# A fused attention kernel gets a new opening: loads reordered, biases transposed beside the token, batch 0 projected by seven products

## The chip, the cores and the metric

The kernel runs on one core of a Trainium2 chip. The metric is the device time of one execution in microseconds, as the median of several runs. A core has five engines that run side by side, each through its own list of instructions in order: TensorE (PE: matmuls and transposes, results into PSUM), ScalarE (ACT: exp, copies), VectorE (DVE: adds, maxima, copies), GpSimd (POOL) and SyncE (SP, which here only issues DMAs). PSUM has eight banks of 128 x 512 fp32. An engine that needs another's result waits on a semaphore.

## The reference

Eight batches of 512 tokens with 512 features, 16 heads of 32. One attention layer with a residual; a condition token of each batch is added to all queries and keys.

```python
Q = _split_heads(x @ Wq.T + bq)
K = _split_heads(x @ Wk.T + bk)
V = _split_heads(x @ Wv.T + bv)
tQ = _split_heads(tokens @ Wq.T + bq)
tK = _split_heads(tokens @ Wk.T + bk)
cQ = Q + tQ
cK = K + tK
scores = jnp.einsum('bhqd,bhkd->bhqk', cQ, cK) / jnp.sqrt(jnp.float32(HEAD_DIM))
attn = jax.nn.softmax(scores, axis=-1)
out = jnp.einsum('bhqk,bhkd->bhqd', attn, V)
...
x = x + _L0_cond_ref(x, cond_1024[:, None, :], ...)
```

Since both the token's and the tokens' projections carry the bias, each query and key gets the token's projection plus twice the bias. The kernel keeps that sum in `tok`.

## The kernel before

Work is cut into 32 steps t: a batch b (8) and a group g of four heads (4 per batch). The operands are fp32. For each t the kernel makes transposed queries and keys (`qkT`, 128 features of the group by 512 tokens), then for each of four row blocks qc the scores of four heads (`row_scores`, four matmuls of 32 x 512 that share the array), their negated row maxima (`row_max_of`, VectorE) and the softmax denominators (`denominators`: four exps on ACT that sum along the row). The maxima of a whole step are split into three bf16 parts (`split_max`, POOL), transposed (`transpose_max`) and added to the transposed scores as a matmul with ones (`exponentials`), whose exps are then multiplied by V (`weighted`).

The order on TensorE, ACT, VectorE and POOL is the order of the text (`manual_schedule`). In the kernel before, that is switched on behind the memsets and loads; only the opening and what follows is written out by hand. Banks are dealt out by the table `TURNS`: each quarter of a step uses one row of it, `advance()` goes to the next row. `one()` deals banks round in the opening.

The loop over t has four quarters. Each has one `exponentials(t, kc)`, one `row_max` of the next step, its `denominators`, and some of the work for the next batch, so that batch b + 1 is loaded, transposed and projected while batch b is in the softmax.

Projections come in two kinds. `project_qk` and `project_v` are four matmuls of 128 x 512 accumulated in one bank. `first_products` and `other_products` do two groups of q or k (or two chunks of V) at once by a Strassen-Winograd scheme: a 2 x 2 block product with seven block products instead of eight, each two matmuls of 256 columns. They need sums of blocks of the weights (`combine_w`, four sums of 128 x 512 per matrix on POOL, into `wc`) and sums of blocks of x (`combine_x`, four sums, on VectorE, into `xc`). `first_products` does products 1, 6, 2 (half) and 7, and ACT copies product 1 (`m1`) out of PSUM ahead of the denominators it is given (`dens`); `other_products` does 4, 5, the other half of 2, and 3. In the kernel before, batch 0 is projected by `project_qk` and `project_v`, and the seven products start with batch 1.

The opening in its order: 28 bf16 matmuls on ones while the loads come; then for c = 0 to 3 a tile of x transposed and a block of w_q transposed (`transpose_w`; even blocks leave PSUM by ACT, odd ones by VectorE); the token transposed (`condT`); projection q of t = 0; `condition("q")` (the token through Wq); w_k's blocks transposed; `condition_end("q")` (turning the result back and adding the biases); projection k with `condition("k")` in between; half of w_v; then four quarters of "burst" (`burst_of_maxima`) in which t = 0's maxima and denominators are interleaved with the other projections of batch 0, the transposes of batch 1's x and the rest of w_v. `combine_w` stands behind the fourth burst. `transpose_x(n)` also loads x tile n + 4. x_7 is transposed by the opening and once more by the loop at t = 0.

Loads before: SyncE issues the token, x_0 to x_3, w_k, the two biases (as 128 x 4, one number at a time), the broadcast bv, w_v; ACT's queue issues w_q.

Of the kernel before, what the change touches and what calls it, by code (L numbers as in the profile page):

```python
# [17 lines left out]
def kernel(  # L18
# [34 lines left out]
    P = 128  # L53
# [38 lines left out]
        (2, 5, 3, 4, 6, 7, 0, 1),  # L92
    ]
# [19 lines left out]
    def load_x(n):  # L113

        if n < B * NS:
            xs[n] = xp.tile([P, D], F32, tag="x", name=f"x_{n}")
            nc.sync.dma_start(xs[n], x[n // NS, n % NS * P : (n % NS + 1) * P, :])
# [14 lines left out]
    for n in ("v", "q", "k"):  # L132
        ws[n] = stage.tile([P, NC, D], F32, tag="w", name=f"w_{n}")

    def load_w(n, w, queue):
        wv = w.rearrange("(c p) d -> p c d", p=P)
        for c in range(NC):
            queue.dma_start(ws[n][:, c, :], wv[:, c, :])

    cond_sb = const.tile([B, D], F32, tag="cond", name="cond_sb")  # L140
    nc.sync.dma_start(cond_sb, cond)
    for n in range(NS):
        load_x(n)
    load_w("q", Wq, nc.scalar)
    load_w("k", Wk, nc.sync)
    bqk = const.tile([P, 2, NC], F32, tag="bqk", name="bqk")
    nc.sync.dma_start(bqk[:, 0, :], bq.rearrange("(c p) -> p c", p=P))
    nc.sync.dma_start(bqk[:, 1, :], bk.rearrange("(c p) -> p c", p=P))
    bvb = const.tile([P, D], F32, tag="bvb", name="bvb")
    nc.sync.dma_start(bvb, bv.rearrange("(o d) -> o d", o=1).broadcast_to([P, D]))  # L150
    load_w("v", Wv, nc.sync)
# [4 lines left out]
    identb = const.tile([P, P], BF16, tag="identb", name="identb")  # L156
    nc.vector.tensor_copy(identb, ident)
    ones = const.tile([P, P], F32, tag="ones", name="ones")
    nc.vector.memset(ones, 1.0)
    onesb = const.tile([P, P], BF16, tag="onesb", name="onesb")  # L160
    nc.vector.memset(onesb, 1.0)
# [6 lines left out]
    nc.vector.memset(condT, 0.0)  # L168
    xc = const.tile([P, 4, 2, HS], F32, tag="xc", name="xc")
# [7 lines left out]
    def transpose_w(n, dc, pt):  # L177

        for cc in range(NC):
            nc.tensor.transpose(  # L180
                pt[:, cc * P : (cc + 1) * P], ws[n][:, dc, cc * P : (cc + 1) * P], ident
            )
        o = wT[n][:, :, dc * P : (dc + 1) * P]
        pv = pt.rearrange("p (c s) -> p c s", c=NC)
        if n == "q":
            if dc % 2:
                nc.vector.tensor_scalar(o, pv, SCALE, None, ALU.mult)
            else:
                nc.scalar.activation(o, pv, AF.Copy, scale=SCALE)
        elif dc % 2:  # L190
            nc.vector.tensor_copy(o, pv)
        else:
            nc.scalar.copy(o, pv)
# [37 lines left out]
    def combine_x(b, half):  # L231

        if b >= B:
            return
        blk = [[xT[b][:, i * 2 : i * 2 + 2, j * HS : (j + 1) * HS] for j in range(2)] for i in range(2)]
        to = [xc[:, i, :, :] for i in range(4)]
        if half == 0:
            nc.vector.tensor_tensor(to[2], blk[1][1], blk[0][1], ALU.subtract)
            nc.vector.tensor_tensor(to[1], to[2], blk[0][0], ALU.add)
        else:  # L240
            nc.vector.tensor_tensor(to[0], blk[0][1], blk[0][0], ALU.subtract)
            nc.vector.tensor_tensor(to[3], blk[1][0], to[1], ALU.subtract)
# [34 lines left out]

    def project_v(n, pt):
        b, sc = divmod(n, NS)
        for cc in range(NC):  # L280
            nc.tensor.matmul(  # L281
                pt,
                xT[b][:, cc, sc * P : (sc + 1) * P],
                wT["v"][:, cc, :],
                start=(cc == 0),
                stop=(cc == NC - 1),
            )
        nc.vector.tensor_copy(vs[b % 2][:, sc, :], pt)
# [60 lines left out]
    def first_products(n, b, u, dens, small, at):  # L349
# [3 lines left out]
        one_, two_ = banks(0), banks(at)  # L353
# [241 lines left out]
    def condition_end(n, pt):  # L595
# [10 lines left out]
        if n == "q":  # L606
            nc.vector.tensor_scalar(bqk[:, 0, :], bqk[:, 0, :], SCALE, None, ALU.mult)
        b1 = bqk[:, i, :].unsqueeze(2).broadcast_to([P, NC, B])
        nc.vector.tensor_tensor(sum4, sum4, b1, ALU.add)
        nc.vector.tensor_tensor(tok[:, i], sum4, b1, ALU.add)  # L610


    ctx.enter_context(
        tc.manual_schedule(
            engines={
                mybir.EngineType.PE,
                mybir.EngineType.Activation,
                mybir.EngineType.DVE,
                mybir.EngineType.Pool,
            }  # L620
        )
    )

    warm = one()
    for _ in range(28):
        nc.tensor.matmul(warm[:, :P], onesb, onesb, start=True, stop=True)
    for c in range(NS):
        transpose_x(c, one())
        transpose_w("q", c, one())
        if c == 1:  # L630
            pc = one()
            for cc in range(NC):
                nc.tensor.transpose(
                    pc[:, cc * B : (cc + 1) * B], cond_sb[:, cc * P : (cc + 1) * P], ident[:B, :B]
                )
            nc.vector.tensor_copy(
                condT[:, :, 0:B], pc[:, : NC * B].rearrange("p (c b) -> p c b", b=B)
            )
    pq = one()
    for cc in range(NC):  # L640
        project_qk_part(0, "q", cc, pq)
    condition("q", one())
    for c in range(NC):
        transpose_w("k", c, one())
    condition_end("q", one())
    project_qk_end(0, "q", pq)
    condition("k", one())
    pk = one()
    for cc in range(NC):
        project_qk_part(0, "k", cc, pk)  # L650
        if cc == 1:
            condition_end("k", one())
    project_qk_end(0, "k", pk)
    transpose_w("v", 0, one())
    transpose_w("v", 1, one())
    turn[0] = 3
# [4 lines left out]
    def burst_of_maxima(t, qc):  # L661
        row_max(t, qc)
        if qc == NS - 1:
            split_max(t)
        denominators(t, qc)

    burst_of_maxima(0, 0)
    project_qk(1, "q", banks(1))
    advance()
    burst_of_maxima(0, 1)  # L670
    project_qk(1, "k", banks(1))
    advance()
    burst_of_maxima(0, 2)
    transpose_w("v", 2, banks(0))
    transpose_w("v", 3, banks(1))
    transpose_x(NS, banks(2))
    project_qk(2, "q", banks(3))
    advance()
    burst_of_maxima(0, 3)
    for n in ("v", "q", "k"):  # L680
        combine_w(n)
    transpose_x(NS + 1, banks(0))
    project_v(0, banks(3))
    transpose_x(NS + 2, banks(1))
    project_qk(2, "k", banks(2))
    advance()
    burst_of_maxima(1, 0)
    project_v(1, banks(3))
    transpose_max(0, banks(1))
    transpose_x(NS + 3, banks(2))  # L690
    project_qk(3, "q", banks(0))
    load_residual(0)
    advance()
# [26 lines left out]
    for t in range(T - 3):  # L720
# [9 lines left out]
        else:  # L730
            transpose_x(t + NS + 3, banks(0), nc.scalar.copy)
            if t:
                project_pair("q", *qk_of, dens, nothing, (1, 3))
            else:
                dens()
                project_qk(3, "k", banks(1))
# [4 lines left out]
        denominators(t + 1, 2)  # L741
        if t:
            invert(t - 1, sums[t - 1])
            weighted(t - 1, banks(0))
        else:
            project_v(2, banks(0))
# [12 lines left out]
        else:  # L759
            dens()  # L760
            project_v(3, banks(0))
# [162 lines left out]
```

## Time and profile before

| | |
|---|---|
| median of the runs | 768.01 us (767.38 to 769.47, 3 runs) |
| profiled execution | 768.58 us |
| its span, first to last instruction | 766.8 us |
| mean granted TensorE clock | 0.997 |
| TensorE busy | 755.3 us, 99% |
| ACT busy | 626.7 us, 82% |
| VectorE busy | 521.6 us, 68% |
| POOL busy | 127.2 us, 17% |
| DMA | 29.76 MB, 38 GB/s over the span |

Times in the views are in microseconds from the start of the span. A line of the timeline has the start, the time covered, the engine, the line of the kernel, the operation, output and inputs, and the shape. An fp32 matmul appears as two records; x8 on a line is four matmuls. The time covered of a TensorE line ends with a modelled tail, so that the next line can start a little earlier; the step from start to start is what a piece of work costs. A window line has from:to, its length, then busy time and instructions of TensorE, of its weight loads (PEld), of VectorE, ACT and POOL, then the granted clock, the DMA share and GB/s.

### The profile page before, as it was taken

The page shows a single profiled execution, that of the slowest core. Times are in us where ns is not written, and L with a number is a line of the kernel's source. Part 1 is how long each engine was busy: PE and PEld are TensorE (multiplying, and loading weights), DVE is VectorE, ACT ScalarE, POOL GpSimd, SP SyncE. Part 2 cuts the span into 40 slices and gives each one's busy share as a digit, 9 for nine tenths or more (in the row PEclk, how much of TensorE's full clock was granted, in tenths as well). Part 3 has the DMA queues.
Part 4 walks back from the last instruction along what each step waited for, and adds up shares of the span by engine and source line. Part 5 has one row for each costly group of instructions (what it writes and reads, how often), then busy time and mean ns, then how long its engine had stood idle before and what let it go on. Part 6 is the DMA issues. An engine that isn't in the chain of part 4 may idle for free.

```text
span 766.8 us, 14247 instructions
## 1 busy us (share of the span) xinstructions
PE 755.3 (99%) x5446; PEld 427.2 (56%) x5446; DVE 521.6 (68%) x720; ACT 626.7 (82%) x1454; POOL 127.2 (17%) x223
## 2 busy tenths in 40 slices
PE   8999999999999999999999999999999999999997
PEld 5444566555656655555655555665555665555332
DVE  3455676676767777677767776777766777667664
ACT  2447898888888888888888888898888988888865
POOL 0063011111011111111111101111110111110120
PEclk9999999999999999999999999999999999999999
DMA  9011011101111110111111011110101111010100
GB/s 307 23 42 29 15 42 42 29 15 42 42 43 42 37 35 15 42 42 43 42 28 43 15 42 42 42 42 12 45 1 29 29 29 28 1 41 16 45 26 28
DMA packets 41571, 29.76 MB, mean 39 GB/s; under 512 B 2840, under 2 KB 35608, under 8 KB 41504
## 3 DMA queue, kind: packets, MB, share of 16 engines
q1 hardware_dynamic: 40656, 27.68, 12.7%
q10 hardware_dynamic: 848, 1.18, 0.5%
q8 instruction: 42, 0.69, 0.4%
q14 instruction: 25, 0.20, 0.1%
HBM read 20.47 MB, written 8.39 MB: 38 GB/s over the span
## 4 chain that ended last, share of the span: by engine, by line
PE 96%; ACT 1%; DVE 1%; DMA 1%; issue 0%; SPq 0%; DVEq 0%
PE psum L324 23%; PE psum L520 15%; PE psum L501 14%; PE psum L419 14%; PE psum L321 12%; PE psum L498 6%; PE psum L255 4%; PE psum L225 2%; PE psum L552 2%; PE psum L281 2%; PE psum L482 1%; ACT e L513 1%; DMA x<-in_x_dram 1%; PE psum L180 1%; ACT e L515 0%
## 5 line engine op out<-in xcount | busy, mean ns | idle before, releaser
L428 DVE TENSOR_REDUCE nmax<-psum 128x2 f32<-128x1024 f32 x256 | 301.8, 1219 | 164.8 <-PE psum L419 164.1
L456 ACT ACTIVATE dead<-psum,nmax 128x512 f32<-128x512 f32 x496 | 334.6, 691 | 23.0 <-DVE nmax L428 23.0
L513 ACT ACTIVATE e<-psum 128x512 f32<-128x512 f32 x270 | 145.8, 595 | 87.3 <-PE psum L501 87.2
L419 PE MATMUL psum<-kT,qT 32*128 32x512 f32 x1024 | 139.0, 598 | 0.3 <-ACT e L515 0.3
L501 PE MATMUL psum<-qT,kT 32*128 32x512 f32 x1024 | 133.2, 591 | 0.0
L515 ACT ACTIVATE e<-psum 128x1024 f32<-128x1024 f32 x121 | 124.9, 1032 | 0.0
L520 PE MATMUL psum<-e,v 128*32 128x512 f32 x1024 | 118.6, 596 | 0.4 <-ACT e L515 0.3
L456 ACT ACTIVATION_READ_ACCUMULATOR dead<-psum,nmax 128x1 f32 x496 | 103.9, 209 | 0.0
L470 POOL CAST split<-nmax 128x16 bf16<-128x16 f32 x32 | 8.1, 253 | 545.0 <-DVE nmax L428 545.0
L419 PEld LDWEIGHTS psum<-kT,qT 32*128 32x128 f32 x1024 | 64.4, 184 | 52.8 <-issue 29.1
L520 PEld LDWEIGHTS psum<-e,v 128*32 128x32 f32 x1024 | 29.5, 109 | 82.9 <-issue 57.9
L498 PE MATMUL psum<-maxT,onesb 3*128 3x512 bf16 x512 | 51.3, 384 | 1.6 <-DVE res L566 0.8
L501 PEld LDWEIGHTS psum<-qT,kT 32*128 32x128 f32 x1024 | 51.2, 185 | 2.5 <-issue 0.2
L577 POOL TENSOR_TENSOR res<-res,xr 128x512 f32<-128x512 f32 x30 | 38.1, 1270 | 66.2 <-DVE res L566 66.2
L498 PEld LDWEIGHTS <-onesb 3*128 3x128 bf16 x512 | 13.4, 91 | 62.2 <-issue 52.6
L542 DVE COPY oT<-psum 128x512 f32<-128x512 f32 x29 | 20.1, 691 | 35.7 <-PE psum L520 35.7
L324 PE MATMUL psum<-xc,wc_q 128*128 128x256 f32 x168 | 43.4, 381 | 0.3 <-ACT e L515 0.3
L321 PE MATMUL psum<-wc_v,xc 128*128 128x256 f32 x168 | 43.3, 380 | 0.0
L324 PE MATMUL psum<-xc,wc_k 128*128 128x256 f32 x168 | 43.2, 380 | 0.0
L129 POOL TENSOR_TENSOR xr<-xr,bvb 128x512 f32<-128x512 f32 x32 | 40.6, 1270 | 0.0
L324 PEld LDWEIGHTS psum<-xT,wT_k 128*128 128x128 f32 x168 | 26.4, 190 | 12.8 <-ACT e L513 10.6
L324 PEld LDWEIGHTS psum<-xc,wc_q 128*128 128x128 f32 x168 | 30.8, 190 | 4.7 <-ACT e L515 1.1
(146 smaller groups left out, 837.5 us busy)
## 6 DMA issues: line engine op xcount, KB each, us to landing
x<-in_x_dram SPq DMA_DIRECT2D x33, 256.0 KB, 2.7
xr<-in_x_dram SPq DMA_DIRECT2D x32, 256.0 KB, 3.1
out_dram<-res SPq DMA_DIRECT2D x31, 256.0 KB, 2.4
w_q<-in_L_cond_Wq_dram ACTq DMA_DIRECT2D x4, 256.0 KB, 4.9
w_k<-in_L_cond_Wk_dram SPq DMA_DIRECT2D x4, 256.0 KB, 5.2
w_v<-in_L_cond_Wv_dram SPq DMA_DIRECT2D x4, 256.0 KB, 5.7
bvb<-in_L_cond_bv_dram SPq DMA_DIRECT2D x1, 256.0 KB, 4.9
out_dram<-res SPq DMA_DIRECT2D x1, 128.0 KB, 1.9
```

What stands on the lines that cost most here:

```text
L129: nc.gpsimd.tensor_tensor(xr[t], xr[t], bias, ALU.add)
L321: nc.tensor.matmul(pt, xb, w, start=(kc == kcs[0]), stop=(kc == kcs[-1]))
L324: nc.tensor.matmul(pt, w, xb, start=(kc == kcs[0]), stop=(kc == kcs[-1]))
L419: nc.tensor.matmul(pt, qkT["q", t][r, qc * P : (qc + 1) * P], qkT["k", t][r, :], start=True, stop=True,)
L428: nc.vector.tensor_reduce(nmax[t][:, qc, pr * 2 : pr * 2 + 2, 0], pt, AX.X, ALU.max, negate=True)
L456: nc.scalar.activation(dead, banks(HG + j), AF.Exp, bias=nmax[t][:, qc, j, :], accum_out=sums[t][:, qc, j, :],)
L498: nc.tensor.matmul(bank[j], onesb[r, :], maxT[t][r, :], start=True, stop=False)
L501: nc.tensor.matmul(bank[j], qkT["k", t][r, kc * P : (kc + 1) * P], qkT["q", t][r, :], start=False, stop=True,)
L513: nc.scalar.activation(e[:, i, :], bank[pr * 2 + i], AF.Exp)
L515: nc.scalar.activation(e, banks(2, 2), AF.Exp)
L520: nc.tensor.matmul(pt[j * HD : (j + 1) * HD, :], vs[b % 2][:, kc, (g * HG + j) * HD : (g * HG + j + 1) * HD], es[t, kc, j // 2][:, j % 2, ...
L577: last.tensor_tensor(y, y, xr.pop(t), ALU.add)
```

## The change

All loads of x stand first and use two queues: SyncE x_0 and x_2, ACT x_1 and x_3. Then SyncE loads the token and the two biases as rows 8, 9 of the same tile, block 0 of w_q, blocks 2 and 3 of w_q, blocks 1 to 3 of w_k, w_v, and the broadcast bv; ACT loads block 0 of w_k and block 1 of w_q. `manual_schedule` is switched on ahead of the loads. One exp on ACT behind its loads brings in the table.

The opening transposes x_0 to x_3 first (two leave by ACT, two by VectorE), then the token with the biases in one set of four transposes, then block 0 of w_q and of w_k and block 1 of w_q; projection q of t = 0 starts with one block of w_q, and projection k with one block of w_k. The other blocks of w_q, w_k and all of w_v follow around the condition. The sums of x's blocks of batch 0 are made on POOL (`combine_x` with `on`), and `combine_w` for q, k and v stands behind the opening's transposes, ahead of the first maxima. `condition_end` adds a ready doubled bias in one step (for k on POOL). Banks in the opening are named one by one (`bank(i)`).

The quarters of t = 0's maxima then do: t = 1's q and k by `project_qk`; groups 2 and 3 of q, and half of k, by seven products; chunks 0 and 2 of V by seven products. In the loop at t = 0 the second half of k's products and the products of V's chunks 1 and 3 take the places of `project_qk(3, "k")`, `project_v(2)` and `project_v(3)`. x_7 is transposed only in the loop. Five rows are added to `TURNS`; `first_products` takes the index of its first bank; `project_v` and `burst_of_maxima` are gone.

```diff
-    def load_x(n):
+    def load_x(n, queue=nc.sync):
...
-    cond_sb = const.tile([B, D], F32, tag="cond", name="cond_sb")
-    nc.sync.dma_start(cond_sb, cond)
-    for n in range(NS):
-        load_x(n)
-    load_w("q", Wq, nc.scalar)
-    load_w("k", Wk, nc.sync)
-    bqk = const.tile([P, 2, NC], F32, tag="bqk", name="bqk")
-    nc.sync.dma_start(bqk[:, 0, :], bq.rearrange("(c p) -> p c", p=P))
-    nc.sync.dma_start(bqk[:, 1, :], bk.rearrange("(c p) -> p c", p=P))
+    load_x(0)
+    load_x(1, nc.scalar)
+    load_x(2)
+    load_x(3, nc.scalar)
+
+    cond_sb = const.tile([B + 2, D], F32, tag="cond", name="cond_sb")
+    nc.sync.dma_start(cond_sb[:B, :], cond)
+    nc.sync.dma_start(cond_sb[B : B + 1, :], bq.rearrange("(o d) -> o d", o=1))
+    nc.sync.dma_start(cond_sb[B + 1 : B + 2, :], bk.rearrange("(o d) -> o d", o=1))
+    load_w("q", Wq, nc.sync, [0])
+    load_w("k", Wk, nc.scalar, [0])
+    load_w("q", Wq, nc.scalar, [1])
+    load_w("q", Wq, nc.sync, [2, 3])
+    load_w("k", Wk, nc.sync, [1, 2, 3])
+    load_w("v", Wv, nc.sync)
     bvb = const.tile([P, D], F32, tag="bvb", name="bvb")
     nc.sync.dma_start(bvb, bv.rearrange("(o d) -> o d", o=1).broadcast_to([P, D]))
-    load_w("v", Wv, nc.sync)
...
+    table = const.tile([P, 1], F32, tag="table", name="table")
+    nc.scalar.activation(table, ones[:, :1], AF.Exp)
...
-    def transpose_w(n, dc, pt):
+    def transpose_w(n, dc, pt, odd=None):
...
-    def combine_x(b, half):
+    def combine_x(b, half, on=nc.vector):
...
-        if n == "q":
-            nc.vector.tensor_scalar(bqk[:, 0, :], bqk[:, 0, :], SCALE, None, ALU.mult)
-        b1 = bqk[:, i, :].unsqueeze(2).broadcast_to([P, NC, B])
-        nc.vector.tensor_tensor(sum4, sum4, b1, ALU.add)
-        nc.vector.tensor_tensor(tok[:, i], sum4, b1, ALU.add)
+        on.tensor_tensor(
+            tok[:, i], sum4, bias2[:, i, :].unsqueeze(2).broadcast_to([P, NC, B]), ALU.add
+        )
...
     for c in range(NS):
-        transpose_x(c, one())
-        transpose_w("q", c, one())
...
+        transpose_x(c, bank(1 + c), nc.scalar.copy if c % 2 else nc.vector.tensor_copy)
+    pc = bank(6)
...
+    nc.vector.tensor_copy(condT[:, :, 0:B], pcv[:, :, 0:B])
+    bias2 = const.tile([P, 2, NC], F32, tag="bias2", name="bias2")
+    nc.vector.tensor_scalar(bias2[:, 0, :], pcv[:, :, B], 2.0 * SCALE, None, ALU.mult)
+    nc.vector.tensor_scalar(bias2[:, 1, :], pcv[:, :, B + 1], 2.0, None, ALU.mult)
+    for half in range(2):
+        combine_x(0, half, nc.gpsimd)
+    transpose_w("q", 0, bank(7), 1)
+    transpose_w("k", 0, bank(1), 0)
+    transpose_w("q", 1, bank(2), 1)
+    pq, pk = bank(5), bank(0)
     for cc in range(NC):
         project_qk_part(0, "q", cc, pq)
...
+    transpose_w("q", 2, bank(3), 0)
+    transpose_w("q", 3, bank(4), 1)
     for cc in range(NC):
         project_qk_part(0, "k", cc, pk)
...
+    transpose_w("k", 1, bank(6), 0)
+    condition("q", bank(7))
+    transpose_w("k", 2, bank(1), 1)
+    transpose_w("k", 3, bank(2), 0)
+    transpose_w("v", 0, bank(3), 1)
+    condition_end("q", bank(4), nc.vector)
+    project_qk_end(0, "q", pq)
+    condition("k", bank(6))
+    transpose_w("v", 1, bank(7), 1)
+    condition_end("k", bank(3), nc.gpsimd)
+    transpose_w("v", 2, bank(1), 0)
     project_qk_end(0, "k", pk)
...
+    transpose_w("v", 3, bank(4), 1)
+    transpose_x(NS, bank(2), nc.scalar.copy)
+    for n in ("q", "k", "v"):
+        combine_w(n)
...
+    turn[0] = 13
+    row_max(0, 0)
+    transpose_x(NS + 1, banks(0), nc.scalar.copy)
+    denominators(0, 0)
+    project_qk(1, "q", banks(3))
     project_qk(1, "k", banks(1))
     advance()
...
+    row_max(0, 1)
+    transpose_x(NS + 2, banks(2), nc.scalar.copy)
+    first_products("q", 0, 1, lambda: denominators(0, 1), nothing, 0, 1)
     advance()
...
+    row_max(0, 2)
+    other_products("q", 0, 1, lambda: denominators(0, 2), nothing, (0, 1))
+    first_products("k", 0, 1, nothing, nothing, 3, 2)
     advance()
...
+    row_max(0, 3)
+    split_max(0)
+    first_products("v", 0, 0, lambda: denominators(0, 3), nothing, 2, 0)
+    advance()
+    row_max(1, 0)
+    transpose_max(0, banks(3), nc.scalar.copy)
+    other_products("v", 0, 0, lambda: denominators(1, 0), nothing, (2, 0))
     load_residual(0)
-    advance()
+    turn[0] = 0
...
-                dens()
-                project_qk(3, "k", banks(1))
+                other_products("k", 0, 1, dens, nothing, (1, 3))
...
-            project_v(2, banks(0))
+            first_products("v", 0, 1, dens, nothing, 1)
...
-            dens()
-            project_v(3, banks(0))
+            other_products("v", 0, 1, dens, nothing, (0, 2))
```

## The prediction

> **What bounds the kernel now.** I read the page from the chain that ended last, then the slices, then the windows of the opening, then TensorE's timeline.
>
> ```profile
> PE 96%; ACT 1%; DVE 1%; DMA 1%; issue 0%; SPq 0%; DVEq 0%
> ...
> PE   8999999999999999999999999999999999999997
> ...
> PEclk9999999999999999999999999999999999999999
> ```
>
> TensorE sets the end: 96% of the chain is its own work, at the full granted clock in every slice, and all that the change leaves alone (t = 1 to the end) is such work. So a microsecond taken out of TensorE's stream or its pauses before t = 1 should come off the end. A slack engine matters only where TensorE waits for it. The windows of the first 40 us show pauses only in the first two rows (7.43 and 8.70 busy of 10), with the DMA engines full there (0.84 and 1.05):
>
> ```profile
> 0.00:10.00 10.00, 7.43 (x63) 6.77 (x64) 3.95 (x12) 2.44 (x3) 0.70 (x6) 1.00 0.84 291
> 10.00:20.00 10.00, 8.70 (x48) 4.28 (x47) 3.95 (x9) 2.35 (x5) 0.00 (x0) 1.00 1.05 322
> 20.00:30.00 10.00, 10.00 (x40) 4.79 (x39) 3.90 (x7) 3.95 (x10) 0.00 (x0) 1.00 0.08 19
> ```
>
> "10.00 busy" hides waits, since modelled ends run on. Starts tell more. TensorE's timeline, opening and after:
>
> ```profile
> 10.71 3.67 PE L255 MATMUL psum<-xT,wT_q 128*128 128x512 f32 x8 [0.44 <-DVE xT L228]
> ...
> 24.58 1.57 PE L419 MATMUL psum<-kT,qT 32*128 32x512 f32 x8
> 26.08 3.70 PE L255 MATMUL psum<-xT,wT_q 128*128 128x512 f32 x8
> 29.71 1.35 PE L419 MATMUL psum<-kT,qT 32*128 32x512 f32 x8
> 30.99 3.70 PE L255 MATMUL psum<-xT,wT_k 128*128 128x512 f32 x8
> 34.62 1.69 PE L419 MATMUL psum<-kT,qT 32*128 32x512 f32 x8
> 36.24 1.09 PE L180 MATMUL psum<-ident,w_v 128*128 128x128 f32 x8
> ...
> 58.91 0.39 PE L498 MATMUL psum<-maxT,onesb 3*128 3x512 bf16 x4
> ...
> 76.34 0.40 PE L498 MATMUL psum<-maxT,onesb 3*128 3x512 bf16 x4
> ```
>
> A score group (L419) takes 0.96 from start to next start when nothing is in its way (60.00 to 60.95 elsewhere in this view); here three take 1.50, 1.28 and 1.62: 1.5 us of waiting for PSUM banks. 58.91 is the start of t = 0's loop, 76.34 its last quarter, from which both kernels issue the same TensorE work. I work out when the changed kernel reaches the second.
>
> **Products.** Eight projections of batch 0 (q and k of head groups 2 and 3; v in four chunks), four matmuls of 128x512 each, go. Each takes 3.53 from start to next start (46.58 to 50.11). In come four pairs of seven products, two matmuls of 256 columns each. The same work on later batches gives the price: two such matmuls follow each other in 0.86 (107.80 to 108.66), 0.97 for the first after scores (84.08 to 85.05), 0.96 for the last before the next group (86.78 to 87.74). A pair is then 14 x 0.43 = 6.02 plus two or four such edges of 0.1, 6.35 on average, against 2 x 3.53 = 7.06: about 0.7 saved, four times 2.8 us. VectorE gets six small adds per pair (0.41 to 0.75) in place of two copies; at 4 to 6.5 us busy of each 10 in this stretch it has room.
>
> **A doubled tile.** Before, x_7 is transposed twice (54.94 and 60.95) and x_11 loaded twice; the changed text transposes it once, in the loop. 0.45 us of TensorE (54.94 to 55.38).
>
> **Opening up to the first scores.** Loads first. Before, x_0 was issued at 1.19, behind cond, and landed 3.5 us later; the four x were transposed from 4.78 to 9.24, interleaved with w_q. Now x goes first on two queues. The DMA carried 0.66 MB by 4.0 us, 1.05 by 5.0, 1.70 by 7.0, 2.1 by 8.0, 2.5 by 9.0 (windows of 1 us). Four x are 1.05 MB: the first two can land by 4.4, when the warm-up ends, the others by 5.3. SyncE's queue then carries cond, the two bias rows, then q0. But the built program makes later issues wait for landings: ACT issues k0 only when x_0 is there (about 4.0), q1 only when x_2 is (5.3); SyncE issues q2 after x_1 and q3 after x_3. By bytes, q0 lands at about 6.2, k0 with q2 at 7.5, q1 with q3 at 8.6. ACT has these issues ahead of its table load, which moves from 2.60 to about 5.7, where nothing covers it: x_1 and x_3 leave PSUM by ACT at about 7.1 and 7.6, done 8.2. That is just ahead of q1. Transposes: x 4.4 to 6.2, cond to 6.5, q0 to 6.95, k0 at 7.6, q1 at 8.6; the first projection starts at 9.05, where it was 10.71.
>
> How long the load holds ACT decides here. The only row is 1.28 us at 2.60, with ACT's next instruction at 6.02 waiting for TensorE. The Trainium skill, "ScalarE: Activation LUTs", What ACT_TABLE_LOAD costs, has 1.283 us as well but adds a drain of about 1.38, 2.66 in all for a switch of sets. By that rule xT is whole at 9.6 and the projection starts at 9.6, 0.55 later. The trace cannot show a drain; nothing runs on ACT before this load, so I take the row, and keep 0.55 for the range.
>
> From 9.05, in order: projection q 3.53, w_q 2 and 3 0.9, projection k 3.53, k1 0.45, condition q 1.0 (14.31 to 15.31), k2, k3, v0 1.35, turning part_q 0.45, condition k 1.0, v1 0.45, a wait of about 0.35 for part_k's copy (0.59 behind condition k, covered by v1 alone), part_k 0.45, v2, v3, x_4 1.35, a wait of about 0.5 for kT (ACT copies v2 first, then kT, 0.48 + 0.76 to the scores against 0.9 of transposes). Sum 15.3: first scores at 24.4 against 24.58, but with v2, v3 and x_4 done, which were 1.35 later on. Gain: 1.5. The biases cost TensorE nothing (the same four transposes, 10 rows for 8), VectorE two ops of 0.16 for bqk's 0.16 and two sums of 0.19; tok for k goes to POOL at about 0.3, inside the wait for kT.
>
> **GpSimd.** Before, its sums of weights ran 45.91 to 61.0; the new opening needs them early:
>
> ```profile
> 50.94 1.26 POOL L209 TENSOR_TENSOR wc_q<-wT_q 128x512 f32<-128x512 f32 x1
> 52.28 1.27 POOL L210 TENSOR_TENSOR wc_q<-wc_q,wT_q 128x512 f32<-128x512 f32 x1
> 53.50 1.27 POOL L211 TENSOR_TENSOR wc_q<-wT_q 128x512 f32<-128x512 f32 x1
> ```
>
> 1.23 from start to start. x's four sums run 8.3 to 13.2, tok for k at 22.9, then twelve sums: q to 28, k to 33, v to 38. First uses, product 6: q at 35, k at 42.5, v at 46.5. Covers of 7 to 9 us; POOL's c1 piece of k and split_max come at 42 and 47, behind all of it. A rule speaks against this: "SBUF — State Buffer", Who interferes with whom, says that a VectorE instruction with two SBUF inputs and a GpSimd one that reads SBUF exclude each other for a whole instruction. By the rule, were every VectorE instruction from 23 to 38 of that kind (about 7 us), v would be done at 45, still in time. The row: POOL's 1.27 did not stretch, nor VectorE's 0.68 copies at 44.61 and 46.95 beside it, all of them reading PSUM, as nearly all here do. I take 0.
>
> **From the scores to t = 0.** Five score groups 4.8, x_5 and x_6 0.9, q1 and k1 7.06, pairs q and v 12.8, first half of k 3.0, maxima 0.23: 28.7. Then waits. Denominators are four of 0.66 on ACT, after the first maximum (1.14). M1's copy ahead of them delays them by 0.3. In the short quarter of v (4.1 us) the last denominators of row block 3 end about 5.0 after its scores' start, and the next scores want these banks (3 and 4): 0.95 us of waiting. The other quarters clear it by 0.5 or more (TensorE 4.6 and 7.0 against 2.9 + 2.7 on ACT with two banks free earlier). In all 29.7; the same addition made for the kernel before gives 33.9 where the trace has 34.3, so I add 0.4: 30.1, t = 0 at 54.5. In t = 0, half k for a projection and halves v for two save 0.8 of the 17.43 to 76.34.
>
> **Sum.** 58.91 - 54.5 + 0.8 = 5.2 us. By parts: products 2.8, x_7 0.45, opening 1.5, bank waits 1.5 less 0.95 = 0.55; 5.3, agreeing within the rounding. The profiled execution took 768.58, span 766.8: I expect span 761.6, 763.4 for it. Its 768.58 lies 0.57 above the median of 768.01, so the forecast of the median is 762.8.
>
> **Rivals.** (1) The sum holds within a microsecond or so: 761.3 to 764.3, chance 0.55. (2) Loads late: the waits of ACT's queue put q1 where w_q's last block was before (about 10.3, landing times of 4.9 to 6.1 us in a loaded queue speak for it; fewer bytes ahead of it speak against). The projection starts at 10.7 or later, the opening's gain is gone but for the order: 764.4 to 765.5. Chance 0.2; it is also the case in which the new order of loads does nothing. (3) ACT bounds the compact quarters: denominators, M1 and maxT queue up and TensorE waits 2 to 4 us more. For it: the three bank waits above. Against it: ACT was busy 3.5 to 5.8 of 10 us here. 764.8 to 766.8, chance 0.12. (4) Loads land as early as their bytes allow and the bank wait is absent: 760.0 to 761.3, chance 0.09. (5) Slower: the weights' sums come late. v's tenth sum must be there at 46.5, 23.6 after the start of the chain, so below 2.3 us each nothing is lost; to lose 7.5 they must take 3.1 us each, twice and a half the row: 771, chance 0.03. Nothing in the trace shows that.
>
> **Numbers.** Chance of faster by more than 0.3% (about what these runs can tell from no change; under 765.7): all of (1) and (4), most of (2), half of (3): 0.89. Within 0.3%: 0.07. Slower: 0.04. Range 760.0 to 766.0: it leaves out the tails of (4) and (3), and (5).
>
> **What would show it.** The first projection near 9, first scores near 24.4, t = 0 near 54.5 and its last quarter near 70.8 on TensorE's timeline; product 6 never waiting for POOL; one wait near 49 for denominators. It is wrong if the projection starts after 10.7, if w_k's or w_q's landing ends a long pause, or if the distance from t = 1 to the end changes.

## The result: 763.6 us for 767.7, and the profile after

The changed kernel takes 763.62 us in the median of 6 runs (762.58 to 765.25), the kernel before 767.72 in the median of its 6 runs. The ratio is 0.9946, with a 95% interval of 0.9932 to 0.9961: 4.1 us faster, with the interval between 3.0 and 5.2. The forecast was 762.8, a gain of 5.2. The profiled execution took 762.58 with a span of 760.8; it is the fastest of the six, 1.0 us under their median, and all views of the changed kernel are of this one execution.

TensorE still sets the end: the changed kernel's page has, for the chain that ended last, by engines:

```profile
PE 96%; ACT 1%; DMA 1%; DVE 0%; issue 0%; DVEq 0%
```

TensorE's timeline of the changed kernel has the places that the prediction named. The waits at 8.89, at 25.32 and inside the line at 49.93, and one of 0.35 us for part_k's copy (not shown), are the waits that the prediction dealt with; its timeline shows no other of that size between the first transposes and t = 0.

```profile
4.34 2.46 PE L251 MATMUL psum<-ident,x 128*128 128x128 f32 x16
...
7.08 0.66 PE L206 MATMUL psum<-ident,w_q 128*128 128x128 f32 x4
8.89 0.63 PE L206 MATMUL psum<-ident,w_k 128*128 128x128 f32 x4 [1.16 <-DMA w_k<-in_L_cond_Wk_dram]
9.56 0.63 PE L206 MATMUL psum<-ident,w_q 128*128 128x128 f32 x4
10.03 3.60 PE L281 MATMUL psum<-xT,wT_q 128*128 128x512 f32 x8
...
25.32 1.14 PE L433 MATMUL psum<-kT,qT 32*128 32x512 f32 x8 [0.39 <-ACT kT L296]
...
47.68 1.03 PE L335 MATMUL psum<-wc_v,xc 128*128 128x256 f32 x4
...
49.93 2.18 PE L433 MATMUL psum<-kT,qT 32*128 32x512 f32 x8
52.04 0.40 PE L496 MATMUL psum<-identb,split 128*128 128x128 bf16 x4
...
55.45 0.40 PE L512 MATMUL psum<-maxT,onesb 3*128 3x512 bf16 x4
...
71.99 0.39 PE L512 MATMUL psum<-maxT,onesb 3*128 3x512 bf16 x4
```

| start of, us | before | forecast | changed |
|---|---|---|---|
| first projection | 10.71 | 9.05 | 10.03 |
| first scores | 24.58 | 24.4 | 25.32 |
| t = 0 | 58.91 | 54.5 | 55.45 |
| t = 0's last quarter | 76.34 | 71.1 | 71.99 |

(The prediction's closing list has 70.8 for the last row; its own sum gives 76.34 - 5.2 = 71.1.)

Everything after the first row follows the forecast to a tenth: 15.29 us from the first projection to the first scores (forecast 15.3), 30.13 on to t = 0 (30.1), 16.54 on to the last quarter (17.43 less 0.8, which is 16.6). The difference, 0.98 us, had arisen before the first projection. From the last quarter on, both kernels do the same TensorE work, and the windows of 100 us agree. Still this rest took 690.46 us before and 688.81 after. The difference lies in one window of each profile, near the end, in which the kernel before was granted 0.91 of the clock (columns as before: TensorE, its weight loads, VectorE, ACT, POOL, granted clock, DMA, GB/s):

```profile
720.00:740.00 20.00, 17.93 (x152) 7.51 (x148) 13.61 (x14) 14.31 (x31) 4.68 (x7) 0.91 0.10 27
```

```profile
715.65:735.65 20.00, 17.95 (x160) 7.47 (x152) 15.03 (x16) 15.03 (x33) 4.69 (x7) 1.00 0.10 28
```

That belongs to one execution and is no gain of the change: the mean clock differs between executions of both kernels, from 0.996 to 1.0. So below I compare kernels by the start of t = 0's last quarter, which I call the marker, and give the times beside it. By the marker the change is worth 4.35 us.

### The profile page after: what moved, and what is told of

Same layout as the page of the kernel before. It is cut to its first block, busy times and chain, and to the rows that moved or that the text cites. A ratio compares the mean times of both kernels' runs of the same rounds, so it can differ in the third digit from the quotient of the medians.

```text
span 760.8 us, 14393 instructions
## 1 busy us (share of the span) xinstructions
PE 750.4 (99%) x5494; PEld 435.9 (57%) x5494; DVE 525.2 (69%) x730; ACT 630.2 (83%) x1462; POOL 132.9 (17%) x229
## 3 DMA queue, kind: packets, MB, share of 16 engines
q1 hardware_dynamic: 39460, 27.42, 12.6%
## 4 chain that ended last, share of the span: by engine, by line
PE 96%; ACT 1%; DMA 1%; DVE 0%; issue 0%; DVEq 0%
PE psum L338 25%; PE psum L534 15%; PE psum L515 15%; PE psum L433 14%; PE psum L335 14%; PE psum L512 6%; PE psum L566 2%; PE psum L251 2%; PE psum L281 2%; PE psum L496 1%; ACT e L527 1%; DMA w_k<-in_L_cond_Wk_dram 1%; PE psum L206 1%; ACT e L529 0%; DMA x<-in_x_dram 0%
## 5 line engine op out<-in xcount | busy, mean ns | idle before, releaser
L335 PE MATMUL psum<-wc_v,xc 128*128 128x256 f32 x192 | 49.4, 380 | 0.0
L338 PE MATMUL psum<-xc,wc_q 128*128 128x256 f32 x180 | 46.4, 380 | 0.3 <-ACT e L529 0.3
L338 PE MATMUL psum<-xc,wc_k 128*128 128x256 f32 x180 | 46.3, 379 | 0.0
L335 PE MATMUL psum<-wT_v,xT 128*128 128x256 f32 x128 | 37.9, 398 | 0.0
L335 PEld LDWEIGHTS psum<-wc_v,xc 128*128 128x128 f32 x192 | 35.4, 190 | 4.3
```

The lines of the kernel that those rows point to most:

```text
L335: nc.tensor.matmul(pt, xb, w, start=(kc == kcs[0]), stop=(kc == kcs[-1]))
L338: nc.tensor.matmul(pt, w, xb, start=(kc == kcs[0]), stop=(kc == kcs[-1]))
```

## The experiments

**Where the gain is.** The first run keeps the new opening and undoes the products.

```diff
-    first_products("q", 0, 1, lambda: denominators(0, 1), nothing, 0, 1)
+    denominators(0, 1)
+    project_qk(2, "q", banks(1))
...
-    other_products("q", 0, 1, lambda: denominators(0, 2), nothing, (0, 1))
-    first_products("k", 0, 1, nothing, nothing, 3, 2)
+    denominators(0, 2)
+    project_qk(3, "q", banks(0))
+    project_qk(2, "k", banks(2))
...
```

> The changed kernel with its new opening, but batch 0 projected as before: each half of a pair of seven products is replaced by one projection of four 128x512 matmuls in the same place, and the sums of x's blocks of batch 0 are left out. Marker in the profile: the start of the exponentials of t = 0's last quarter, 71.99 us in the changed kernel. Theory (TensorE's stream is the bound, a pair of products saves 0.7 us of it): 2.8 us more TensorE work, less 0.3 because the short quarter grows from 4.3 to 4.6 us and waits less for its banks; marker at 74.3 to 74.8, time 2.3 to 2.8 above the changed kernel. Rival (ACT or the bank waits bound these quarters, so that shorter TensorE work bought little): marker at 72.5 to 73.5.

Measured: 766.38 us (ratio to the kernel before 0.9985, 0.9974 to 0.9996), marker at 74.53. TensorE's timeline of this run:

```profile
9.81 3.60 PE L281 MATMUL psum<-xT,wT_q 128*128 128x512 f32 x8
...
74.53 0.40 PE L524 MATMUL psum<-maxT,onesb 3*128 3x512 bf16 x4
```

From the first projection to the marker it is 64.72 us, against 61.96 in the changed kernel, so the products are worth 2.76 us. That is net: the wait for banks ahead of t = 0 is 0.64 us here (the scores at 51.57 are followed only at 53.28) where it is 1.04 in the changed kernel, so the products take about 3.2 us off TensorE's work and give 0.4 back in that wait. The rest of the change (the opening, the one transpose of x_7 less, the other banks) is then worth 1.6 us of the marker and about 1.3 us of the time.

The second run keeps the new order on TensorE and undoes the order of the loads.

```diff
-    load_x(0)
-    load_x(1, nc.scalar)
...
+    nc.sync.dma_start(cond_sb[:B, :], cond)
+    for n in range(NS):
+        load_x(n)
+    load_w("q", Wq, nc.scalar)
...
```

> The changed kernel with the loads in the order and on the queues of the kernel before (the token and x on SyncE, w_q on ACT's queue, biases, w_k, bv and w_v on SyncE), the biases still as rows. Theory (order of landing sets the start): x_3 lands near 9 and w_k's first block, which stands ahead of the first projection in the text, not before 10.5 to 11.5; first projection at 11 to 12.5 instead of 10.03, marker 1 to 2.5 later (73 to 74.5). Rival (the DMA engines are full anyway and the same bytes are there by then): first projection within 0.4 of 10.03.

Measured: 766.03 us, first projection at 12.96, marker at 74.92, both 2.93 later than in the changed kernel. The direction is the theory's, the size somewhat above its range. TensorE's timeline of this run shows the last of x and the blocks behind it:

```profile
8.19 1.97 PE L245 MATMUL psum<-ident,x 128*128 128x128 f32 x8 [0.59 <-DMA x<-in_x_dram]
10.09 0.60 PE L630 MATMUL psum<-ident,cond_sb 10*128 10x10 f32 x4
10.62 1.12 PE L200 MATMUL psum<-ident,w_q 128*128 128x128 f32 x4
11.52 1.06 PE L200 MATMUL psum<-ident,w_k 128*128 128x128 f32 x4
...
12.96 3.60 PE L275 MATMUL psum<-xT,wT_q 128*128 128x512 f32 x8
```

With the old loads, the new text is later than the old one (10.71): TensorE asks for all of x first, and x_3 lands only at 8.8. But landings are not all of it. From its first transpose to 12.6 us TensorE works at about half its pace: a set of four transposes takes 0.90 from start to start (10.62 to 11.52), where it takes 0.44 to 0.49 in the changed kernel, and one transpose of x has a median of 421 ns against 273. The granted clock in the windows is 1.00 all the while, so that row does not show it. At the full pace, x_3, the token and the three blocks (block 0 of w_k lands at 9.5) are 2.1 us of transposes, and the projection would start near 11.0, an estimate from these numbers: about 1 us of the 2.93 is the landing, about 2 us the slow pace. What sets that pace is not shown; TensorE had stood idle for 1.12 us ahead of x, longer than in any other profiled execution here, and the median of 20 runs is no better than the profiled one. So the new order of the opening does not pay with the old loads; the new loads under the old order were not run.

**Where the missing microsecond went.** The chain that ended last, in the changed kernel's first 30 us (start, length, what):

```profile
0.74 3.46 DMA x<-in_x_dram
4.22 4.54 DMA w_k<-in_L_cond_Wk_dram
8.76 0.14 issue
8.89 0.63 PE psum L206 x4
```

and ACT's timeline, which issues that load:

```profile
0.73 0.90 ACTq L123 DMA_DIRECT2D x<-in_x_dram  x2
4.22 0.34 ACTq L144 DMA_DIRECT2D w_k<-in_L_cond_Wk_dram  x1
5.52 0.34 ACTq L144 DMA_DIRECT2D w_q<-in_L_cond_Wq_dram  x1
5.88 1.28 ACT L193 ACT_TABLE_LOAD   x1 [5.88 <-DMA x<-in_x_dram]
7.18 0.20 ACT L193 ACTIVATE table<-ones 128x1 f32<-128x1 f32 x1
```

Block 0 of w_k is issued when x_0 has landed, at 4.22, and then takes 4.5 us, to 8.76; the forecast was 3.5, from 4.0 to 7.5. Its landing is 1.3 us late, and that of block 1 of w_q behind it (9.43, forecast 8.6) about 0.8. If the wait ahead of the issue is at fault, an earlier issue should bring the blocks in earlier. The third run puts the small loads behind the blocks; the built program then issues the blocks without a wait.

```diff
-    nc.sync.dma_start(cond_sb[:B, :], cond)
-    nc.sync.dma_start(cond_sb[B : B + 1, :], bq.rearrange("(o d) -> o d", o=1))
-    nc.sync.dma_start(cond_sb[B + 1 : B + 2, :], bk.rearrange("(o d) -> o d", o=1))
     load_w("q", Wq, nc.sync, [0])
     load_w("k", Wk, nc.scalar, [0])
     load_w("q", Wq, nc.scalar, [1])
+    nc.sync.dma_start(cond_sb[:B, :], cond)
+    nc.sync.dma_start(cond_sb[B : B + 1, :], bq.rearrange("(o d) -> o d", o=1))
+    nc.sync.dma_start(cond_sb[B + 1 : B + 2, :], bk.rearrange("(o d) -> o d", o=1))
...
```

> The changed kernel with the three small loads (token and biases) issued behind block 0 of w_q and blocks 0 and 1 of w_k and w_q instead of ahead of them, so that these blocks' issues no longer wait for x_0 and x_2 to land; the token's transposes stand behind the first projection. Theory A (0.95 us of the forecast was lost because block 0 of w_k was issued only at 4.22, behind the landing of x_0): the blocks are issued before 3 us, land by 7.7, the table load is over by 4.5, first projection at 8.1 to 8.7 instead of 10.03, marker 1.3 to 1.9 earlier (70.1 to 70.7). Theory B (the DMA engines' bytes set the landing): the blocks land near 9 whatever the issue, first projection after 9.5, marker less than 0.5 earlier.

Measured: 761.62 us (ratio 0.9921, 0.9896 to 0.9946), first projection at 8.42, marker at 70.90. TensorE's timeline of this run:

```profile
4.45 2.36 PE L251 MATMUL psum<-ident,x 128*128 128x128 f32 x16 [0.23 <-DMA x<-in_x_dram]
6.85 0.66 PE L206 MATMUL psum<-ident,w_q 128*128 128x128 f32 x4
7.34 0.60 PE L206 MATMUL psum<-ident,w_k 128*128 128x128 f32 x4
7.96 0.63 PE L206 MATMUL psum<-ident,w_q 128*128 128x128 f32 x4
8.42 3.63 PE L281 MATMUL psum<-xT,wT_q 128*128 128x512 f32 x8
11.98 0.41 PE L644 MATMUL psum<-ident,cond_sb 10*128 10x10 f32 x4
...
70.90 0.39 PE L512 MATMUL psum<-maxT,onesb 3*128 3x512 bf16 x4
```

The blocks, issued at 1.65 and 2.13, land at 7.2 and 7.8, and theory A holds for the projection; theory B, that they land near 9 whatever the issue, is out. The marker gains 1.09 of the 1.61, less than theory A's 1.3 to 1.9: the token's transposes, 0.34, now stand behind the projection where they had lain in the wait, and a smaller part is lost up to the second projection. The rate of the DMA engines differs too. In the changed kernel they moved 217 GB/s from 6 to 7 us and 301 from 7 to 8, though busy for 0.89 and 1.03 of the time; with the early blocks they moved 379 and 383. So they did not stand still between issues; what slowed them is not shown.

This run moved the small loads too, so they could have been the brake themselves. A further run left the text as it was and put only them on GpSimd's queue.

> The changed kernel with only the token's and the biases' loads moved, from SyncE's queue to GpSimd's, behind the identity matrix; everything else, the token's transposes too, stands where it stood. It separates two readings of the run with early blocks. Reading A (the issues of block 0 of w_k and block 1 of w_q waited for x_0 and x_2 to land, because the small loads stood between in the count of outstanding loads): these blocks are issued before 3 us again and land by 8, first projection at 8.2 to 9.0. Start of t = 0's last quarter then 1.0 to 1.8 before the changed kernel's 71.99, provided the token lands by 6.5; a GpSimd load that lands later takes up to 0.5 of it back. Reading C (the small rows slow the engines down whenever they come ahead of the blocks): first projection at 9.6 or later.

Measured: 763.17 us, first projection at 10.50, marker at 72.53. By the expectation's numbers that is reading C, but the blocks were not what held the projection up. They were issued at 1.66 and 2.15, and all three were transposed one after the other from 8.97 with no wait (TensorE's timeline of this run):

```profile
4.93 3.65 PE L251 MATMUL psum<-ident,x 128*128 128x128 f32 x16 [0.71 <-DMA x<-in_x_dram]
...
8.97 0.65 PE L206 MATMUL psum<-ident,w_q 128*128 128x128 f32 x4
```

Up to 8.6 TensorE was busy with x, which had landed by 6.3: it worked at the slow pace of the run with the old loads, 421 ns a transpose for all sixteen. The last of the rows that are transposed with the token landed only at 8.5. In the last new kernel below, which has the same loads, x was done by 7.2, and the wait for the token is named (its TensorE timeline):

```profile
8.53 0.38 PE L636 MATMUL psum<-ident,cond_sb 10*128 10x10 f32 x4 [1.30 <-DMA cond_sb<-in_L_cond_bk_dram]
```

So the token's 16 KB and two rows of 2 KB, issued by GpSimd before 3.2 us, landed at 7.0 and, the rows, at 8.2 to 8.5 (both runs). The blocks landed at 8.0 (w_k) and 9.0 (w_q): earlier than in the changed kernel (8.8 and 9.4), but not by 8 as reading A has it, and later than in the run with early blocks (7.2 and 7.8), where they were issued at the same times. From 2 to 3 us the DMA engines moved 74 GB/s here and 193 there. That speaks for reading C; but block 2 of w_q was also issued at 2.12 instead of 5.59 and took its share. So the pair does not separate the readings, and whether the wait for issue or the small rows cost more stays open. Shown is that this order of loads, the small ones behind the blocks on SyncE's queue, brings the blocks in 1.6 us earlier, and that an early issue buys nothing while the token and its rows come late.

**The bank wait.** Score groups elsewhere in this stretch take 1.07 from start to start; at 49.93 it is 2.11, a wait of 1.04. Prediction: 0.95, for the denominators in banks 3 and 4. The fourth run gives the next scores other banks.

```diff
-        (5, 0, 6, 7, 1, 2, 3, 4),
+        (5, 0, 3, 4, 6, 7, 1, 2),
```

> The changed kernel with other banks for one quarter only: the scores of t = 1's row block 0 go to banks 6, 7, 1, 2 instead of 1, 2, 3, 4, and that quarter's other results to 3 and 4. Theory (the 1.06 us wait at 49.93 is for the denominators of row block 3 to leave banks 3 and 4): the wait goes, and t = 0 starts 0.7 to 1.06 earlier, up to 0.3 of it given back at the first exponentials; marker at 71.0 to 71.4. Rival (ACT itself is late by then, and the wait moves to the exponentials of t = 0): marker at 71.8 or later.

Measured: 764.25 us, marker at 72.08 with the first projection at 10.28, so 61.80 between them instead of 61.96. That is the rival's case, though not yet its reason: the wait is gone from the scores and turns up at t = 0's first exponentials (TensorE's timeline of this run):

```profile
50.18 1.14 PE L433 MATMUL psum<-kT,qT 32*128 32x512 f32 x8
51.25 0.40 PE L496 MATMUL psum<-identb,split 128*128 128x128 bf16 x4
...
54.66 0.39 PE L512 MATMUL psum<-maxT,onesb 3*128 3x512 bf16 x1
55.53 0.39 PE L512 MATMUL psum<-maxT,onesb 3*128 3x512 bf16 x3 [0.49 <-ACT dead L470]
```

The second bank of these exponentials is one in which a late denominator now lies. The quarter's chain (scores 1.1, maximum 1.2, four denominators 2.7: 5.0 us) is longer than its TensorE work (4.29, from 45.64 to 49.93); it costs time where one of its last two banks is asked for first. The fifth run therefore leaves that row as it was and turns the order of banks in the quarter before.

```diff
-        (0, 1, 5, 2, 6, 7, 3, 4),
+        (0, 1, 5, 2, 3, 4, 6, 7),
         (5, 0, 6, 7, 1, 2, 3, 4),
```

> The changed kernel with one row of the bank table altered: the scores of row block 3 lie in banks 3, 4, 6, 7 instead of 6, 7, 3, 4, so that the denominators that end last leave banks 6 and 7, while the next scores keep 1, 2, 3, 4. Theory (the quarter has a chain of scores, maximum and four denominators of 5.2 us in all against 4.3 to 4.4 us of TensorE, and it costs time only where the last two of its banks are asked for next; in the bank change tried before, the first exponentials asked for them): neither the next scores nor the exponentials wait, and from the first projection to the start of t = 0's last quarter it takes 60.9 to 61.2 us, where the changed kernel takes 61.96. Rival (ACT is late whatever the banks, so the wait turns up again behind): 61.7 or more.

Measured: 762.79 us; from the first projection (10.72) to the marker (71.65) 60.93 us, 1.03 less than in the changed kernel. Neither place waits (TensorE's timeline of this run):

```profile
50.62 1.14 PE L433 MATMUL psum<-kT,qT 32*128 32x512 f32 x8
51.70 0.40 PE L496 MATMUL psum<-identb,split 128*128 128x128 bf16 x4
...
55.11 0.40 PE L512 MATMUL psum<-maxT,onesb 3*128 3x512 bf16 x4
...
71.65 0.39 PE L512 MATMUL psum<-maxT,onesb 3*128 3x512 bf16 x4
```

ACT does the same work in the same order in all three. The wait belonged to the order of the banks, not to how much work ACT had.

**GpSimd's cover.** Two runs put idle sums ahead of w_v's.

```diff
+        if n == "v":
+            for _ in range(6):
+                nc.gpsimd.tensor_tensor(extra, wT["q"][:, 0, :], wT["q"][:, 1, :], ALU.add)
         combine_w(n)
```

> The changed kernel with six sums of 128x512 more on GpSimd (results not used) ahead of w_v's four sums: 7.4 us more in its chain. Theory (the sums have 7 to 9 us of cover): w_v's second sum is there at 45.5, product 6 of V starts at 47.7; from the first projection to t = 0's last quarter 61.9 to 62.2, as in the changed kernel (61.96). Rival (GpSimd and VectorE exclude each other, or the cover is less than worked out): 63 or more.

Measured: 61.97 from first projection to marker (762.69 us in one run): nothing is lost. In the changed kernel itself the second sums (GpSimd's timeline) are there long before product 6 starts at 36.28 (q), 43.59 (k) and 47.68 (v):

```profile
25.58 1.27 POOL L236 TENSOR_TENSOR wc_q<-wc_q,wT_q 128x512 f32<-128x512 f32 x1
...
30.59 1.27 POOL L236 TENSOR_TENSOR wc_k<-wc_k,wT_k 128x512 f32<-128x512 f32 x1
...
35.61 1.27 POOL L236 TENSOR_TENSOR wc_v<-wc_v,wT_v 128x512 f32<-128x512 f32 x1
```

> As the run before, with twelve sums more, 14.8 us. Theory: w_v's second sum is there at 52.9, product 6 waits for it about 5 us, the wait of 1.06 us for banks that comes behind it is then covered; from the first projection to t = 0's last quarter 65.5 to 67. Rival (something else covers it): under 63.

Measured: 774.33 us in one run; 70.31 us from first projection to marker, above the range. The wait itself is as worked out, 5.15 us, but what follows is slow (TensorE's timeline of this run; the first two lines are from its opening):

```profile
7.42 0.60 PE L206 MATMUL psum<-ident,w_k 128*128 128x128 f32 x4
10.98 1.09 PE L206 MATMUL psum<-ident,w_q 128*128 128x128 f32 x4 [2.96 <-DMA w_q<-in_L_cond_Wq_dram]
...
55.92 2.07 PE L335 MATMUL psum<-wc_v,xc 128*128 128x256 f32 x4 [5.15 <-POOL wc_v L236]
57.79 1.06 PE L335 MATMUL psum<-wT_v,xT 128*128 128x256 f32 x2
58.64 1.91 PE L335 MATMUL psum<-wc_v,xc 128*128 128x256 f32 x4
```

The same matmuls take 1.03 in the changed kernel; the three lines from 55.92 to the next scores at 60.48 cost 4.56 us where they cost 2.25 there. The granted clock was half from shortly before the end of the pause on: 0.52 from 55 to 56 us, 0.50 from 56 to 61. The same befell this execution's opening, in which w_q's block landed at 10.85: the clock was 0.83 in the mean from 10 to 11 us and 0.50 from 11 to 14, and the first projection took 1.1 us more. One of these windows, with the granted clock behind GpSimd's column:

```profile
11.00:12.00 1.00, 1.00 (x5) 1.00 (x6) 0.00 (x0) 0.00 (x0) 1.00 (x2) 0.50 1.06 404
```

The idle sums stand behind all of that opening, so it is no effect of theirs; without it the twelve sums cost 7.2 us: 5.3 of wait and 2.3 of slow clock, less 0.4 of the bank wait.

**A version that beats both.** Early blocks, the turned banks, and two moves for the wait of 0.5 us at the first scores: ACT copies the keys ahead of w_v's block 2, and x_5 is transposed ahead of the scores.

```diff
-    transpose_w("v", 2, bank(1), 0)
     project_qk_end(0, "k", pk)
+    transpose_w("v", 2, bank(1), 0)
     transpose_w("v", 3, bank(4), 1)
     transpose_x(NS, bank(2), nc.scalar.copy)
+    transpose_x(NS + 1, bank(5), nc.scalar.copy)
...
     row_max(0, 0)
-    transpose_x(NS + 1, banks(0), nc.scalar.copy)
```

> Blocks issued early (as in the run with early blocks) and the bank row just described, and two more moves: ACT copies t = 0's keys ahead of w_v's block 2, and x_5 is transposed ahead of the first scores (in bank 5), into the wait of 0.5 us for the keys. Theory: the gains add, 1.1 for the blocks, 1.0 for the banks, 0.5 for the wait; start of t = 0's last quarter at 69.2 to 69.7 (71.99 in the changed kernel), time 760 to 760.8. Rival (they overlap: ACT gets the keys' copy, x_4's and x_5's copies and the first denominators in a row, and delays the first quarter): 70.0 or later.

Measured: 760.41 us (760.34 to 760.46), ratio to the kernel before 0.991 (0.9896 to 0.9925), marker at 69.75. Its TensorE timeline:

```profile
8.74 3.61 PE L281 MATMUL psum<-xT,wT_q 128*128 128x512 f32 x8
...
69.75 0.40 PE L512 MATMUL psum<-maxT,onesb 3*128 3x512 bf16 x4
```

From the first projection to the marker it is 61.01 us where the run with early blocks alone has 62.48: the turned banks and the two moves bring 1.47 of the 1.5 forecast, so these gains add. The marker lies 0.05 us beyond its range because the first projection began 0.3 us later than in the run with early blocks alone. This kernel is 0.9% faster than the one before, and its interval lies clear of the changed kernel's.

Last, the same moves with the token on GpSimd's queue, and the changed kernel once more.

> As the run before, with the bank row, the keys ahead of w_v's block 2, and x_5 ahead of the first scores. Theory: against the best version so far the token's four transposes (0.35 us) fall into the wait for the blocks instead of behind the first projection, so up to 0.35 us less: time 760.0 to 760.5, start of the last quarter at 69.3 to 69.8. Rival: the token by GpSimd's queue lands late and is itself waited for: 760.5 to 761.5.

> The changed kernel itself, beside the others on one chip. Its first projection began between 9.8 and 10.7 us (once 11.9) in kernels that share its loads, and near 8.5 in the two with early blocks, whose times also lay within 0.7 us of each other where the others spread over 2 to 4. Theory (the landing of the blocks that wait for issue is what varies): times spread over 2 us or more here, those of the two runs above over less than 1. Rival (the spread belongs to the chip at that hour): the spreads are alike.

Measured: 761.35 us for the first, the rival's case: the last of the token's rows lands at 8.4 and is waited for, as the line shown above says. The changed kernel again took 763.03 (762.43 to 765.59), a spread of 3.2 us, where the two beside it spread over 0.35 and 0.3. The theory's numbers came out, and it fits that the first projection of kernels with the changed kernel's loads was profiled anywhere from 9.81 to 11.86. But the landing as the cause is not shown. Three of the four executions lie within 0.74 us; the fourth, 765.59, had a mean granted clock of 0.996 where they had 0.999, and 0.003 of 761 us is 2.3 us, so the clock is a rival. The kernel with the turned banks has the changed kernel's loads and spread over only 0.9 us in four runs, and the kernel before spread over 2.4 beside these runs.

## Why the prediction was right, and where it was off

- **TensorE as the bound, products.** The bound was right. The forecast was 2.8 us less TensorE work; undoing the products costs 2.76, but the bank wait shrinks by 0.4 with them undone, so the work itself is about 3.2 us less: 0.8 a pair where the prediction had 0.7. That the stretches below still came out to a tenth is in part two errors that cancel: the pairs were cheaper and the score groups dearer than forecast.
- **From the first projection to the marker.** Three stretches forecast as 15.3, 30.1 and 16.6 us, measured 15.29, 30.13, 16.54. The waits for part_k's copy and for the keys, and the bank wait (0.95, measured 1.04), lie where they were put. Score groups of the opening took 1.07 instead of 0.96, which the 0.4 added after the same sum for the kernel before covered.
- **The step that was mis-sized: "By bytes, q0 lands at about 6.2, k0 with q2 at 7.5, q1 with q3 at 8.6."** The issue of k0 at 4.0 was right (4.22), and q0 landed at 6.3, but k0 took until 8.76 and q1 until 9.43, so the projection began at 10.03 instead of 9.05. The prediction counted on the bytes that the kernel before had moved, 2.1 MB by 8 us and 2.5 by 9; the changed kernel had moved 1.94 and 2.29. Why its engines were slower from 6 to 8 us is open. Which block is late differs from one profiled execution to the next: in three of the six later ones with these loads (the other banks, the twelve sums, the changed kernel again) k0 landed at 7.1 to 7.5, as forecast, and q1 was waited for; but q1 landed at 9.2 to 10.9 in all of them. Up to the first scores the opening gained 0.6 us (24.58 to 25.32, with 1.35 us of later transposes done) where 1.5 was forecast. That was half of rival 2, the late loads; its size, a projection at 10.7 or later, did not come in this execution but did in two of the later ones (10.72 and 11.86). With a start that differs by 2 us between executions, coming within a microsecond of it was in part luck.
- **The time, and some luck.** The forecast for the profiled execution was a span of 761.6; it came out at 760.8 although the marker was 0.9 late, because 768.58 held the 1.65 us of lower clock near the end that the forecast carried along. The prediction read the row of nines as the full clock in every slice; a nine starts at 0.90. Some sums slipped too, without weight: the parts from the scores to t = 0 add up to 28.8, not 28.7, and three halves at its own price save 1.05 us in t = 0, not 0.8 (measured 0.89).
- **ACT's table load.** The row of 1.28 us was right and the drain does not show: the load ran from 5.88 to 7.16, the next ACT instruction began at 7.18, x left PSUM by 8.34, and none of it was waited for, since w_k's block was later. What a switch between two sets costs no run here shows.
- **GpSimd.** The sums took 1.26 each beside VectorE and cost nothing; rival 5 was rightly small, and six sums more changed nothing. Its price counted only the wait, though: after a pause of 5.15 us the slow clock cost 2.3 us more.
- **ACT as the new bound (rival 3).** TensorE waited for ACT only where the prediction had worked it out: part_k, the keys and the bank wait.

## What to carry to other kernels

In an opening, count which loads wait for earlier loads' landings before they are issued, and put the blocks that TensorE asks for first among those that need not wait; here three small loads (16 KB and twice 2 KB) moved behind such blocks brought the marker 1.1 us forward. A wait for a PSUM bank can be gone when the banks that come free last are not the ones asked for first, without taking work from any engine; look one stage on before calling it gone. Where the order of the text changes, look at the loads again: the new text on the old loads started its first projection 2.3 us after the old text. And one profiled opening is one draw: with the same loads the first projection began anywhere from 9.8 to 11.9 us.

## What the runs showed of the hardware that was not expected

A pause of TensorE costs more than its length. After 2.96 us without work the granted clock was 0.83 in the mean from 10 to 11 us, 0.50 from 11 to 14 and 0.96 from 14 to 15, together half the clock for about 3.4 us (an estimate from these shares); after 5.15 us matmuls took 2.07 where they take 1.03. The Trainium skill, "TensorE: Matmul & The Clock Gate", Part 1: The HAM clock gate, puts the fall to half the rate after an idle window of about 3.4 us that runs freely; the pause of 2.96 us here was slightly shorter and was enough. The changed kernel's pause of 1.16 us in the profile did not lower the clock.

The first transposes of a kernel can run at a slow pace that the granted clock does not show. A transpose of x took 421 ns from the first to the last in two profiled executions (the old loads; the small loads on GpSimd's queue) and 273 ns from the first on in three others (the old products, the six and the twelve sums); the rest changed over in between. The windows have 1.00 for the clock in all of them. The two slow ones had the longest pauses between the warm-up matmuls and x, 1.12 and 0.71 us, but a pause of 0.46 us came with the full pace and one of 0.12 us with five slow transposes, so the pause alone does not settle it.

Small loads from GpSimd's queue, issued between 1.46 and 3.15 us, landed at 7.0 (16 KB) and 8.2 to 8.5 (rows of 2 KB), while the same loads issued by SyncE at 1.66 to 2.6 in the changed kernel were there by 6.74; fewer of the blocks had been issued beside them there.
